# A transformer block's last batch: output tiles, the last pair's softmax sums, and the output gate, in another order

## The chip, the cores and the metric

The kernel runs on one core of one Trainium2 chip. The metric is the device time of one execution in microseconds (us), the median of several runs of the same program.

## What is computed

The reference is one block with adaptive layer norm, on an input of 8 batches, 1024 rows and 256 columns:

```python
h = _layernorm(x, axis=-1) * (1 + ca) + sa
x = x + ga * _L0_attn_ref(h, w_qkv, w_o)        # 16 heads of 64 columns
h = _layernorm(x, axis=-1) * (1 + cb) + sb
x = x + gb * _L0_ffn_ref(h, router_w, router_b, w1, b1, w2, b2)
```

`sa, ca, ga, sb, cb, gb` are six rows of 256 numbers for each batch. The attention is softmax(q k / 8) v for each head, then one product with `w_o`. The second part routes: a softmax over 8 experts for each of the 8192 rows, and each expert takes its 512 highest rows, applies two layers to them and adds the result, weighted by the score, to the output. So no expert can begin before every row of every batch has its score: the search for each expert's threshold needs all of them.

## The kernel before

**Attention.** A unit is one batch, one pair of heads and one half of 512 queries: 8 batches, 8 pairs, 2 halves, 128 units (`NSU`). Each has eight chunks of 128 keys. The work is written out by hand in steps `g`, four for a unit, in a loop (L732 on) that issues for each step: the subtraction of the row maxima (`subtract`, L425), the score products of a later unit (`scores_mm`, L360), exponentials (`exp_of`, L428) and value products (`values_mm`, L431) of a unit six steps back. Other work is put into these steps by `at(g, where, f, ...)` (L247), with places named load, m1, post, pool and m2, and is issued by `run` (L250). Each engine executes its instructions in the order issued; the SP queue too.

**Sums.** GpSimd adds up the eight exponential tiles of a unit (`add_up`, L449); `den_out` (L462) multiplies the sum by a matrix of ones (`den_mm`, L468: four 32-row products into one PSUM tile) and `den_store` (L478) copies it out and stores it to DRAM. When both halves of a pair are there, `den_load` (L492) reads the sums back as 128 rows, `den_inv` (L498) takes reciprocals and stores them, `den_spread` (L506) loads each as a broadcast over 64 partitions (`rb`), and `den_mul` (L514) multiplies the pair's transposed output `oT` by them, on GpSimd; on VectorE for the last pair of the last batch. `oT` goes to DRAM and comes back by tiles of 128 rows (`ot`), except for the last two pairs of the last batch (`at_hand`, L460), which stay in SBUF.

**Output of a batch, a tile of 128 rows at a time.** `out_proj` (L542): 16 products, over eight pairs, into one PSUM tile. `out_add` (L554): times the gate `ga` (L558, VectorE, `mods[b][:, 0]`), plus the residual (L559), store, statistics (L116, L117). `out_norm` (L563): 1/sqrt on GpSimd (`rstd_of`, L106, L108), scale (L571), times 1 + cb (L572) and plus sb (L573) on GpSimd. `out_turn` (L576): two tiles are transposed by products with the identity, in 64-column halves, and copied out (L590). `out_route` (L593): the logits of both tiles and their maximum. `out_exp` (L610), `out_score` (L618) and `out_store` (L628): the softmax over experts, a copy into `scores`, and a store of the row. For batches 0 to 6 these steps lie between the attention steps of the next batch.

**The last batch** has no attention to lie under, and is written out behind the loop (L771 to L823). For the last unit, `den_mm` isn't preceded by GpSimd's adding: four products for each chunk stand between the value products (L755 to L758). Behind the loop stand, in this order: the store, load, reciprocal and spread of the last pair's sums, the load of `mods` and of the residuals `xs` (L771 to L786); for each of eight tiles, the products of pairs 0 to 6 (L802 to L807); the product of the last pair's `oT` with the reciprocals (L808); for each tile, pair 7 (L809); and then one loop over the tiles, in which `out_add` of tile s, `out_norm` of tile s - 1 and the routing steps of earlier tiles follow each other:

```python
        for s in range(NT + 5):
            if s < NT:
                out_add(b, s, pos[s])
            if 1 <= s < NT + 1:
                out_norm(b, s - 1)
```

`last_load` (L641) loads `ot` for the last batch, six pairs of a tile at a time, at steps 515 and 516.

**Behind it**: the weights of four experts are loaded (`load_expert`), the scores are transposed (L889), and the threshold search runs 15 rounds on VectorE and TensorE (L899 to L924; L904 counts). Then the experts (L1083 to L1101).

Of the kernel before, what the change touches and what calls it, by code (L numbers as in the profile page):

```python
# [28 lines left out]
F32 = mybir.dt.float32  # L29
# [3 lines left out]
ALU = mybir.AluOpType  # L33
# [4 lines left out]
P = 128  # L38
# [4 lines left out]
def adaln_block(  # L43
# [15 lines left out]
    nc = tc.nc  # L59
# [418 lines left out]
    def den_store(u, pd):  # L478
        b, p, h = unit(u)
        den = small.tile([P, QH], F32, tag="den", name=f"den{u}", bufs=2)  # L480
        nc.scalar.copy(den, pd)
        if h == 0:
            den_d[b, p] = dram.tile([2, S], F32, name=f"den_d{b}_{p}")
        nc.sync.dma_start(
            den_d[b, p][:, h * QB : (h + 1) * QB].rearrange("j (i q) -> j i q", i=2),
            den[::32, :],
        )


    dens = {}  # L490
# [22 lines left out]

    def den_mul(b, p):  # L514
        oT = oTs.pop((b, p))
        if (b, p) == (B - 1, NP - 1):
            nc.vector.tensor_mul(oT, oT, dens.pop((b, p)))
        else:
            nc.gpsimd.tensor_tensor(oT, oT, dens.pop((b, p)), ALU.mult)  # L519
        if (b, p) in at_hand:  # L520
            at_hand[b, p] = oT
        else:
            nc.sync.dma_start(oT_d[b][p], oT)


    o_x, o_h, o_t = {}, {}, {}
# [49 lines left out]
    def out_turn(pool, b, t, tag="mm"):  # L576

        n = f"{b}_{t}"
        pt = pool.tile([P, 2, KC, P], F32, tag=tag, name=f"pth{n}")
        for i in range(2):  # L580
            h2 = o_h[b, t + i]
            for k in range(KC):
                for m in range(2):
                    c0 = k * P + m * N
                    nc.tensor.matmul(
                        pt[m * N : (m + 1) * N, i, k, :], h2[:, c0 : c0 + N], ident,
                        start=True, stop=True,
                    )
        h2T = small.tile([P, 2, KC, P], F32, tag="h2T", name=f"h2T{n}", bufs=1)
        nc.scalar.copy(h2T, pt)  # L590
        o_x[b, t] = h2T
# [44 lines left out]
    def gates(b):  # L636
        nc.sync.dma_start(
            rows_d[b * S : (b + 1) * S, ROW:], gb_d[b : b + 1, :].to_broadcast([S, D])
        )

    def last_load(t):  # L641
        b = B - 1
        o_t[b, t] = work.tile([P, NP - 2, P], F32, tag="p", name=f"ot{b}_{t}", bufs=PB)
        nc.sync.dma_start(
            o_t[b, t], oT_d[b][: NP - 2, :, t * P : (t + 1) * P].rearrange("n p s -> p n s")
        )
# [18 lines left out]
    for b in range(B):  # L665
        for p in range(NP):
            P0 = 8 * (b * NP + p)
            for i, g in enumerate((-7, -6, -5, -2)):
                if P0:
                    at(P0 + g, "m1", qk_task, b, p, i)  # L670
            if p % 2 == 0:
                for t, g in enumerate((-9, -3, -1, 5)):
                    if P0 or g > 0:
                        at(P0 + g, "m1", v_task, b, p // 2, t)
            if (b, p) == (B - 1, NP - 1):
                continue

            at(P0 + 17, "load", den_load, b, p)
            at(P0 + 18, "post", den_inv, b, p)
            at(P0 + 19, "load", den_spread, b, p)  # L680
            at(P0 + 20, "pool", den_mul, b, p)
        if b + 1 < B:
            if b + 2 < B:
                for t in range(NT // 2):
                    ln_task(b + 2, t, free_slot(64 * (b + 1) + 39 + 4 * t, True))
            for t in range(NT):
                g = free_slot(64 * (b + 1) + 19 + 4 * t, True)
                at(g - 2, "load", out_load, b, t)
                at(g, "m2", out_proj, ps_m, b, t)
                at(g + 1, "pool", out_norm, b, t)  # L690
                if t % 2:
                    g = free_slot(g + 2, True)
                    at(g, "m2", out_turn, ps_m, b, t - 1)
                    g = free_slot(g + 1)
                    at(g, "m2", out_route, ps_m, b, t - 1)
                    at(g + 1, "post", out_exp, b, t - 1)
                    at(g + 2, "post", out_score, b, t - 1)
                    at(g + 3, "pool", out_store, b, t - 1)
    for u in range(NSU):
        at(4 * u + 4, "m1", max_rows, u)  # L700
        if u < NSU - 1:
            at(4 * u + 12, "m2", den_out, u)
    for b in range(B):
        at(64 * b + 30, "load", gates, b)
    for i in range(2):
        at(2 + i, "m2", mod_rows, i)
    for t in range(NT):
        at(4 * NSU + (3 if t < NT // 2 else 4), "load", last_load, t)

    with tc.manual_schedule():  # L710
        first_loads()
# [20 lines left out]
        while g < 4 * NSU + LAG or steps:  # L732
            u, gm = divmod(g, 4)
            run(g, "load")
            if gm == 1 and 0 < u <= NSU:
                max_spread(u - 1)
            u1, gm1 = divmod(g - LAG + 1, 4)
            late = [(u1, 2 * gm1 + i) for i in range(2) if 0 <= u1 < NSU]

            for uc in late[: 1 if gm == 3 else 2]:  # L740
                subtract(*uc)
            if 0 <= u < NSU:
                for c in (2 * gm, 2 * gm + 1):
                    scores_out(u, c, scores_mm(u, c))
            if gm == 3 and late:
                subtract(*late[1])
            run(g, "m1")
            run(g, "post")
            for uc in late:
                exp_of(*uc)  # L750
            u1, gm1 = divmod(g - LAG, 4)
            if 0 <= u1 < NSU:
                for c in (2 * gm1, 2 * gm1 + 1):
                    values_mm(u1, c)
                    if u1 == NSU - 1:  # L755
                        if c == 0:
                            pd_last = ps_s.tile([P, QH], F32, tag="s", name="pd_last")
                        den_mm(pd_last, probs.pop((u1, c)), start=(c == 0), stop=(c == NT - 1))  # L758
                if gm1 == 3:
                    values_out(u1)  # L760
                if u1 < NSU - 1:
                    add_up(u1, gm1)
            if gm == 3 and 0 <= u < NSU:
                max_turn(u)
                split_max(u)
            run(g, "pool")
            run(g, "m2")
            g += 1


        b = B - 1  # L771
        den_store(NSU - 1, pd_last)
        den_load(b, NP - 1)
        den_inv(b, NP - 1)
        den_spread(b, NP - 1)
        mods[b] = work.tile([P, 3, D], F32, tag="mod", name=f"mod{b}", bufs=1)
        nc.sync.dma_start(
            mods[b].rearrange("p m d -> p (m d)"), mod_d[b : b + 1, :].to_broadcast([P, 3 * D])
        )
        for i in range(2):  # L780
            xs = work.tile([P, 4, D], F32, tag="p", name=f"xs{i}", bufs=PB)
            nc.sync.dma_start(
                xs, x[b, i * 4 * P : (i + 1) * 4 * P, :].rearrange("(t p) d -> p t d", p=P)
            )
            for t in range(4):
                o_x[b, 4 * i + t] = xs[:, t : t + 1, :]  # L786

        pos = []
        for pool, tag, n in (
            (ps_s, "s", 2), (ps_b, "less", 2), (ps_m, "mm", 1), (ps_av, "av", 1), (ps_s, "s", 2)  # L790
        ):
            po = pool.tile([P, n, 512], F32, tag=tag, name=f"po_last{len(pos)}")
            pos += [po[:, i, :D] for i in range(n)]

        def add_pair(t, p, src):
            for m in range(2):
                nc.tensor.matmul(
                    pos[t][m * N : (m + 1) * N, :], src[:, m * N : (m + 1) * N],
                    wo[:, p, :], start=(p == 0), stop=(p == NP - 1),
                )  # L800

        for t in range(NT):  # L802
            for p in range(NP - 1):
                if p < NP - 2:
                    add_pair(t, p, o_t[b, t][:, p, :])
                else:
                    add_pair(t, p, at_hand[b, p][:, t * P : (t + 1) * P])  # L807
        den_mul(b, NP - 1)  # L808
        for t in range(NT):  # L809
            add_pair(t, NP - 1, at_hand[b, NP - 1][:, t * P : (t + 1) * P])  # L810
        for s in range(NT + 5):
            if s < NT:
                out_add(b, s, pos[s])
            if 1 <= s < NT + 1:
                out_norm(b, s - 1)
            if s % 2 == 0 and 2 <= s < NT + 2:
                out_turn(*((ps_s, b, 0, "s") if s == 2 else (ps_m, b, s - 2)))
            if s % 2 and 3 <= s < NT + 3:
                out_route(ps_b, b, s - 3, tag="less")
                out_exp(b, s - 3)  # L820
            if s % 2 == 0 and 4 <= s < NT + 4:
                out_score(b, s - 4)
                out_store(b, s - 4)  # L823
    assert not steps, sorted(steps)
    attn.close()

# [306 lines left out]
```

## Time and profile before

| what | us |
|---|---|
| median of 3 runs | 3599.44 (3599.09 to 3600.59) |
| the profiled execution | 3597.83 |
| its span, first to last instruction | 3596.1 |
| TensorE busy in it | 3450.2 (96%) |
| VectorE, ScalarE, GpSimd busy | 2859.3, 2438.7, 2652.1 |
| last instruction of the attention loop's value products | 3212.6 |
| first count of the threshold search (L904) | 3272.6 |
| first product of the experts (L1049) | 3349.6 |

Times inside the execution are counted from the first instruction of the span. In the profile PE is TensorE's products, PEld its loading of weights, DVE VectorE, ACT ScalarE, POOL GpSimd, SP the queue that issues most transfers; "SPq" lines are its issues. An arrow names what was written and what was read, with buffer numbers left out. In the timeline a line gives start, duration, engine, line, operation, operands and count, and in brackets the idle time before it and what ended that. Instructions of the same kind that follow each other are merged into one line. A table by stretches gives for each one its length, then the busy time and number of instructions of each engine, the TensorE clock granted as a share of full speed, the busy share of the transfer engines and GB/s. The waits give who waited for whom, the total, how often, and the longest.

### The profile page before, as it was taken

To read this page: it belongs to the slowest core of one execution; us is meant where nothing else is said; L and a number is where in the kernel's file an instruction comes from. 1 tells how busy PE (TensorE), PEld (TensorE's weight loads), DVE (VectorE), ACT (ScalarE), POOL (GpSimd) and SP (SyncE) were. 2 spreads that over 40 slices of the span, in tenths; PEclk is the share of its full clock that TensorE was granted. 3 is DMA by queue.
4 is the path that set the end of the run, shared out by engine and by line. 5 is a ranking of instruction groups with operands and counts; after the bars stand their busy time and mean duration, and the time that the engine had idled before them with its cause. 6 is when DMAs were issued, how large, how long until landed. Compare 5 with 4: busy or idle time off the path is not lost. (4 is left out here: it accounts for less than half of the span.)

```text
span 3596.1 us, 54368 instructions
## 1 busy us (share of the span) xinstructions
PE 3450.2 (96%) x20718; PEld 1454.7 (40%) x20718; DVE 2859.3 (80%) x3618; ACT 2438.7 (68%) x2996; POOL 2652.1 (74%) x1537
## 2 busy tenths in 40 slices
PE   7999999999999999999999999999999999993898
PEld 3333333343433434334433343344433434442566
DVE  5888888888888888888888888988888888867432
ACT  4777777777777777777777777777777777750111
POOL 2778778888888887978788888887888788752233
PEclk9999999999999999999999999999999999995899
DMA  3020012011130112111211112111211112133342
GB/s 78 13 42 31 25 32 67 30 45 45 51 59 29 50 57 56 34 40 45 66 53 31 48 50 63 31 42 53 59 44 44 41 44 63 46 92 129 93 101 43
DMA packets 189653, 185.40 MB, mean 52 GB/s; under 512 B 48952, under 2 KB 167240, under 8 KB 189264
## 3 DMA queue, kind: packets, MB, share of 16 engines
q1 hardware_dynamic: 173616, 160.29, 16.3%
q0 software_dynamic: 7168, 12.72, 1.8%
q10 hardware_dynamic: 8608, 8.92, 0.8%
q8 instruction: 163, 2.67, 0.3%
q14 instruction: 98, 0.80, 0.1%
HBM read 127.06 MB, written 63.21 MB: 53 GB/s over the span
## 5 line engine op out<-in xcount | busy, mean ns | idle before, releaser
L457 POOL TENSOR_TENSOR acc<-acc,p 128x1024 f32<-128x1024 f32 x762 | 1805.3, 2369 | 362.4 <-ACT p L429 329.1
L376 ACT COPY p<-s 128x1024 f32<-128x1024 f32 x1024 | 995.8, 1018 | 419.1 <-PE s L367 412.1
L426 DVE TENSOR_TENSOR p<-p,less 128x1024 f32<-128x1024 f32 x1024 | 1206.7, 1210 | 32.6 <-PE less L423 30.1
L381 DVE TENSOR_TENSOR top<-top,s 128x1024 f32<-128x1024 f32 x768 | 936.8, 1220 | 276.3 <-ACT p L376 236.0
L429 ACT ACTIVATE p<-p 128x1024 f32<-128x1024 f32 x1024 | 1041.7, 1057 | 73.7 <-DVE p L426 73.3
L367 PE MATMUL s<-qk,qk 64*128 64x512 f32 x4096 | 1024.7, 612 | 34.0 <-DVE parts L404 31.0
L438 PE MATMUL av<-p,v 128*64 128x512 f32 x4096 | 967.2, 593 | 1.8 <-ACT oT L447 1.8
L367 PEld LDWEIGHTS s<-qk,qk 64*128 64x128 f32 x4096 | 358.8, 186 | 527.5 <-issue 240.9
L332 PE MATMUL pq<-hT,wq 128*64 128x512 f32 x2048 | 498.5, 608 | 2.7 <-ACT v L354 2.1
L438 PEld LDWEIGHTS av<-p,v 128*64 128x64 f32 x4096 | 280.6, 137 | 461.4 <-issue 366.2
L454 POOL TENSOR_TENSOR acc<-p,p 128x1024 f32<-128x1024 f32 x127 | 301.6, 2375 | 178.1 <-ACT p L429 178.1
L332 PEld LDWEIGHTS pq<-hT,wq 128*64 128x64 f32 x2048 | 124.8, 136 | 342.2 <-issue 210.8
L349 PE MATMUL pv<-wq,hT 128*64 128x256 f32 x2048 | 249.3, 386 | 0.7 <-ACT qk L337 0.7
L1053 ACT ACTIVATE h<-ph,b_sb 128x512 f32<-128x512 f32 (+1 forms) x72 | 46.0, 639 | 263.5 <-PE ph L1049 263.5
L396 DVE TENSOR_REDUCE tt<-tt 128x8 f32<-128x1024 f32 x128 | 157.4, 1230 | 69.9 <-PE tt L388 69.8
L548 PE MATMUL po<-wo,ot 128*64 128x256 f32 x1792 | 205.7, 382 | 0.0
L349 PEld LDWEIGHTS pv<-wq,hT 128*64 128x64 f32 x2048 | 135.7, 136 | 153.2 <-issue 65.9
L381 DVE TENSOR_TENSOR top<-p,s 128x1024 f32<-128x1024 f32 x128 | 155.8, 1217 | 14.0 <-ACT p L376 14.0
L388 PEld LDWEIGHTS tt<-ident,top 128*128 128x128 f32 x1024 | 109.6, 140 | 106.6 <-DVE top L381 105.8
L519 POOL TENSOR_TENSOR oT<-oT,rb 128x1024 f32<-128x1024 f32 x63 | 150.0, 2380 | 3.7 <-DMA rb<-rden_d 3.7
L548 PEld LDWEIGHTS po<-wo,ot 128*64 128x64 f32 x1792 | 123.5, 137 | 66.1 <-issue 9.4
L388 PE MATMUL tt<-ident,top 128*128 128x128 f32 x1024 | 139.9, 280 | 2.6 <-DVE top L381 2.6
(169 smaller groups left out, 2293.4 us busy)
## 6 DMA issues: line engine op xcount, KB each, us to landing
rb<-rden_d SPq DMA_DIRECT2D x128, 256.0 KB
oT_d<-oT SPq DMA_DIRECT2D x62, 512.0 KB
ot<-oT_d SPq DMA_DIRECT2D x56, 512.0 KB
rows_d<-row SPq DMA_DIRECT2D x64, 132.0 KB
rows_d<-gb_d SPq DMA_DIRECT2D x8, 1024.0 KB
w<-in_L_ffn_w_dram ACTq DMA_DIRECT2D x8, 1024.0 KB
w<-in_L_ffn_w_dram SPq DMA_DIRECT2D x8, 1024.0 KB
lnx<-in_L_attn_inputs_dram SPq DMA_DIRECT2D x28, 256.0 KB
```

The source lines that it names most:

```text
L332: nc.tensor.matmul(pq[m * N : (m + 1) * N, :], wq_of(k, a, 2 * p + m), hTs[b][:, k, sl], start=(k == 0), stop=(k == KC - 1),)
L349: nc.tensor.matmul(pv[m * N : (m + 1) * N, i, :], hTs[b][:, k, t0 : t0 + N], wq_of(k, 2, 4 * g, 4), start=(k == 0), stop=(k == KC - 1),)
L367: nc.tensor.matmul(ps[:, j, :], kt[r, c * P : (c + 1) * P], qt[r, h * QB : (h + 1) * QB], start=True, stop=True,)
L376: nc.scalar.copy(probs[u, c], ps)
L381: nc.vector.tensor_tensor(tops[u], probs[u, 0] if c == 1 else tops[u], ps, ALU.max)
L388: nc.tensor.transpose(turned[u][:, 4 * j + t, :], top[:, j, t * P : (t + 1) * P], ident)
L426: nc.vector.tensor_tensor(probs[u, c], probs[u, c], less[u], ALU.add)
L429: nc.scalar.activation(probs[u, c], probs[u, c], AF.Exp)
L438: nc.tensor.matmul(avs[u][j * N : (j + 1) * N, :], v[:, c, hh * N : (hh + 1) * N], pT[:, j, :], start=(c == 0), stop=(c == NT - 1),)
L454: nc.gpsimd.tensor_tensor(sums[u], pts[0], pts[1], ALU.add)
L457: nc.gpsimd.tensor_tensor(sums[u], sums[u], pt, ALU.add)
L548: nc.tensor.matmul(po[m * N : (m + 1) * N, :], ot[:, p, m * N : (m + 1) * N], wo[:, p, :], start=(p == 0), stop=(p == NP - 1),)
```

## The change

The loop of attention steps is the same up to step 508. In the last steps and behind the loop:

- The last unit's chunks 0 to 3 are added up by GpSimd like those of other units; the products with ones for chunks 4 to 7 and for that sum stand behind all value products, in another PSUM pool. The unit before gets its `den_out` one step earlier.
- The sums of the last pair are handled in halves of 512 queries: store, load, reciprocal, store, broadcast load and product for each half. Half 0 is issued on SP, half 1 on ScalarE's queue. Both products are VectorE's.
- `mods` of the last batch is loaded at step 510, and VectorE multiplies the output weights `wo` by the gate in two halves at step 516; the multiplication by the gate for each tile is gone.
- The scores of the tiles 6 and 7 of batch 6 are computed at step 516 instead of an earlier one (behind the last subtractions).
- Tiles 0 to 3 get pairs 0 to 6, then pair 7; each later tile gets its eight pairs in one piece, between the residuals, norms, turns, routes and softmaxes of earlier tiles, in an order written out as a list. Odd tiles' products with 1 + cb and sums with sb are VectorE's, even tiles' GpSimd's. The last batch's transposes are whole 128x128 ones.

```diff
+        if (b, p) == (B - 1, NP - 1):
+            dst = den_d[b, p, h] = dram.tile([2, QB], F32, name=f"den_d{b}_{p}_{h}")
...
+        eng = nc.scalar if u == NSU - 1 else nc.sync
+        eng.dma_start(dst.rearrange("j (i q) -> j i q", i=2), den[::32, :])
...
+    def last_load_den(h):
+        d = last_d[h] = small.tile([P, 2 * QB // P], F32, tag="dq", name=f"dq_last{h}", bufs=2)
+        (nc.scalar if h else nc.sync).dma_start(
+            d, den_d[B - 1, NP - 1, h].rearrange("j s -> (j s)").rearrange("(p c) -> p c", p=P)
+        )
+
+    def last_inv(h):
+        eng = nc.scalar if h else nc.sync
+        nc.vector.reciprocal(last_d[h], last_d[h])
+        rd = dram.tile([2, QB], F32, name=f"rden_last{h}")
+        eng.dma_start(
+            rd.rearrange("j s -> (j s)").rearrange("(p c) -> p c", p=P), last_d[h]
+        )
+        t = last_d[h] = work.tile([P, QB], F32, tag="p", name=f"rb_last{h}", bufs=PB)
+        for j in range(2):
+            eng.dma_start(
+                t[j * N : (j + 1) * N, :], rd[j : j + 1, :].to_broadcast([N, QB])
+            )
+
+    def last_mul(h):
+        half = oTs[B - 1, NP - 1][:, h * QB : (h + 1) * QB]
+        nc.vector.tensor_mul(half, half, last_d[h])
...
+                if b == B - 1:
+                    nc.tensor.transpose(pt[:, i, k, :], h2[:, k * P : (k + 1) * P], ident)
+                    continue
...
+    def last_gates():
+        n = NP // 2
+        for i in range(2):
+            w = wo[:, i * n : (i + 1) * n, :]
+            nc.vector.tensor_tensor(
+                w, w, mods[B - 1][:, 0, :].unsqueeze(1).to_broadcast([P, n, D]), ALU.mult
+            )
...
-            at(4 * u + 12, "m2", den_out, u)
+            at(4 * u + (12 if u < NSU - 2 else 11), "m2", den_out, u)
...
+    at(4 * NSU - 2, "load", last_mods)
...
+    at(4 * NSU + 4, "load", last_load_den, 0)
+    at(4 * NSU + 4, "pool", last_gates)
+    at(4 * NSU + 5, "post", last_inv, 0)
...
-                    if u1 == NSU - 1:
-                        if c == 0:
-                            pd_last = ps_s.tile([P, QH], F32, tag="s", name="pd_last")
-                        den_mm(pd_last, probs.pop((u1, c)), start=(c == 0), stop=(c == NT - 1))
...
-                if u1 < NSU - 1:
+                if u1 < NSU - 1 or gm1 < 2:
                     add_up(u1, gm1)
...
+        pd_last = ps_m.tile([P, QH], F32, tag="mm", name="pd_last")
+        for c in range(4, NT):
+            den_mm(pd_last, probs.pop((NSU - 1, c)), start=(c == 4), stop=False)
+        den_mm(pd_last, sums.pop(NSU - 1), start=False)
+        den_store(NSU - 1, pd_last)
+        last_load_den(1)
+        last_inv(1)
...
+        def add_x(t):
+            x1 = o_x[b, t]
+            nc.vector.tensor_add(x1[:, 0, :], x1[:, 0, :], pos[t])
+            nc.sync.dma_start(out[b, t * P : (t + 1) * P, :], x1[:, 0, :])
+            mv = stats_of(small, x1, 1, f"b{b}_{t}")
+            o_h[b, t] = mv, rstd_of(small, mv, 1, f"b{b}_{t}")
+
+        def norm(t):
...
+            eng = nc.vector if t % 2 else nc.gpsimd
+            eng.tensor_tensor(h2, h2, mods[b][:, 2, :], ALU.mult)
+            eng.tensor_tensor(h2, h2, mods[b][:, 1, :], ALU.add)
...
+        half = NT // 2
+        for t in range(half):
+            add_pairs(t, 0, NP - 1)
+        last_mul(0)
+        for t in range(half):
+            add_pairs(t, NP - 1, NP)
+        last_mul(1)
+        for f, *args in (
+            (add_x, 0), (add_x, 1), (norm, 0), (add_pairs, 4, 0, NP), (add_x, 2), (norm, 1),
+            (add_x, 3), (norm, 2), (add_pairs, 5, 0, NP), (turn, 0), (norm, 3), (add_x, 4),
+            (route, 0), (norm, 4), (add_pairs, 6, 0, NP), (turn, 2), (add_x, 5), (norm, 5),
+            (score, 0), (route, 2), (add_pairs, 7, 0, NP), (turn, 4), (add_x, 6), (norm, 6),
+            (score, 2), (add_x, 7), (route, 4), (norm, 7), (score, 4), (turn, 6), (route, 6),
+            (score, 6),
+        ):
+            f(*args)
```

`add_pairs(t, p0, p1)` issues the products of tile t for pairs p0 to p1 - 1 (the old `add_pair` in a loop over pairs); `turn` and `route` are `out_turn` and `out_route` in the pool of the score products; `score` is `out_exp`, `out_score` and `out_store` one behind the other.

## The prediction, made before the changed kernel ran

> **What bounds the kernel now.** I read the forty-slice view first: TensorE is full until slice 36, then 3, 8, 9, 8, so the change can only act in the tail of the attention part. Next the busy times by stretch:
>
> ```profile
> 3200.00:3213.00 13.00, 12.99 (x104) 3.10 (x104) 6.17 (x10) 7.20 (x10) 3.77 (x4) 1.00 0.78 195
> 3213.00:3237.00 24.00, 24.00 (x226) 16.00 (x224) 1.48 (x2) 0.57 (x2) 0.00 (x0) 1.00 0.55 143
> 3241.00:3247.00 6.00, 1.29 (x14) 1.01 (x16) 4.37 (x12) 0.00 (x0) 4.33 (x9) 0.74 0.19 63
> 3247.00:3254.00 7.00, 3.59 (x38) 2.53 (x34) 4.81 (x16) 1.08 (x3) 4.70 (x11) 0.50 0.18 59
> ```
>
> The columns are TensorE, weight loads, VectorE, ScalarE, GpSimd, then clock, DMA share, GB/s. From 3213 to 3237 TensorE alone works (the output products of eight tiles); from 3241 VectorE and GpSimd work and TensorE idles, half-clocked. Two phases stand one behind the other. The waits say what joins them:
>
> ```profile
> DVE at L558 <- PE po_last L797: 10.8, 1, 10.8
> PEld pth L585 <- POOL row L573: 14.0, 7, 2.9
> DVE oT L517 <- DMA rb<-rden_d: 6.1, 1, 6.1
> ```
>
> The first residual waits until every tile has pairs 0 to 6, though its operands are long there; then each transpose waits for GpSimd. The timeline gives the anchors:
>
> ```profile
> 3203.89 9.52 SPq L644 DMA_DIRECT2D ot<-oT_d  x8
> 3218.39 0.32 SPq L494 DMA_DIRECT2D dq<-den_d  x1
> 3226.34 1.23 DVE L517 TENSOR_TENSOR oT<-oT,rb 128x1024 f32<-128x1024 f32 x1 [6.13 <-DMA rb<-rden_d]
> 3238.37 0.42 DVE L558 TENSOR_TENSOR at<-po_last,mod 128x256 f32<-128x256 f32 x1 [10.81 <-PE po_last L797]
> 3242.04 0.72 DVE L559 TENSOR_TENSOR xs<-xs,at 128x256 f32<-128x256 f32 x1
> 3272.64 0.75 DVE L904 TENSOR_SCALAR_CACHE_REDUCE above<-sc,cand 128x512 f32<-128x512 f32 x1
> ```
>
> First residual at 3238.37, first count of the threshold search at 3272.64. Everything behind 3272.64 (323.5 us) is the same work before and after, so the question is where this anchor goes.
>
> **What the Trainium skill says.** "SBUF — State Buffer", section "Who interferes with whom": a VectorE instruction with two SBUF inputs and a GpSimd instruction that reads SBUF exclude each other for a whole instruction. The trace agrees: L559 takes 0.42 us alone and 0.72 across GpSimd's L572. "TensorE: Matmul & The Clock Gate", section "Part 1": an idle window of about 3.4 us halves the clock, a busy one restores it. The trace agrees: 1.00 falls to 0.50 at about 3244, 3 us after the dense products, and returns at 3353.1, 3.5 us after the experts' products begin at 3349.6. "DMA: Bandwidth & Descriptors", section "Issuing engines are not separate DMA queues": transfers of two queues run on the same 16 engines; a second queue saves issue time only. No row here shows it for the last pair.
>
> **The change part by part.**
>
> *Sums behind the values.* Eight groups of den_mm stood between the values at about 0.57 us each (start to start in the timeline, 3201.01 to 3201.58); now five groups of 0.5 (p4 to p7, and the GpSimd sum of p0 to p3) stand behind them. The values then wait for the exponentials instead: VectorE's last subtraction ends near 3205.6 (the score instructions, 0.76, moved behind it; before 3206.24), the last exponential near 3206.9, the last value product near 3207.9, the sums near 3210.4. GpSimd takes on three adds of 2.38 us, 3201.1 to 3208.4, before its oT product (then to 3210.8, before 3210.3). So the output products start near 3210.5 instead of 3213.06.
>
> *Gates in the output weights.* Two VectorE products of 128x1024, 1.23 us each by L517's row, before the first output product; they remove eight 0.42 us multiplications (L558) and turn L559's two-SBUF-input add into one that reads PSUM. Nobody waits if they end by 3210.5: uncontended 3208.9. With the lock against GpSimd's adds and oT product each may wait up to one 2.37 us instruction: up to 3213. I take 3211; a late start is covered, because TensorE waits at pair 7 anyway (next step). Without that cover it costs up to 2.5 us. The `mod` load moved to group 510 is one 0.57 us issue on SP, which was idle until 3196.
>
> *Halves on two queues.* SP's order is now: four ot loads, den store of half 0, four ot loads, dq load, reciprocal's store, rb, row stores, xs. The ot loads fill SP and the engines (DMA share about 1.2 from 3207 to 3217; the packets end near 3218.3), so the dq load of half 0, issued near 3214, lands behind them, near 3218.6. From here the trace of before has the whole chain: dq issue 3218.39, landed 3219.96, rb issue 3221.68, product 3226.34. So: reciprocal 3218.9, rb issue 3220.6. Both rb halves (ScalarE's queue carries the other, and its reciprocal stands behind half 0's on VectorE) together are the bytes of the old rb: 2.9 us of packets, 3221.9 to 3224.4 for half 0. The added waits: on SP, half 0's reciprocal store also waits for the landing of half 1's den store (they share a completion counter in the built program; ScalarE issues that near 3211, landed near 3213: no wait, but rb, rows and xs stand behind it); on ScalarE, four waits for transfers up to 3221.8, with nothing behind them before the first copy of a transpose near 3233; on VectorE, half 1's reciprocal stands ahead of product 0, its load issued near 3213 and landed near 3215. Product 0 is 0.62 us (half of L517): ends 3225.2. TensorE has done four tiles of pairs 0 to 6 (3.02 us each in the timeline, 12.1 together) by 3222.6 to 3224, waits 1 to 3 us, and starts pair 7 at 3225.3. Two tiles of it (0.86) and the 0.4 us that L558 saw behind its last product: 3226.6. xs must be there as well: SP issues it after rb and two row stores, near 3222.6; its packets follow those of rb and rows: first half landed near 3227.3. First residual **3227.3** instead of 3238.37: 11.1 us gained. Bounds: 3225.2 if dq isn't last behind the slowest engine and xs overlaps; 3230 if xs needs the 8.1 us from the first rb packet that it took before.
>
> *Tile by tile.* TensorE's remaining work is in VectorE's shadow: tiles 4 and 5 (3.45 each) end 7.4 us behind tile 3's pair 7; turn (0.55 now, whole transposes), copy (0.6), route (0.6) fit between. VectorE, with the timeline's pitches: add, statistics, aggregate 1.03 a tile; scale 0.3; an odd tile's two products 0.92, up to 1.5 against GpSimd's pair (0.75 each); logits 0.4 and scores 0.85 a pair; mean to rstd and back 1.05 (3246.28 to 3247.30). Laid out in the order of the built program from residual 0: tiles 0 to 3 normalised at 9.25 (two lock waits), residuals 4 and 5 from 9.25 and 11.6 (1.4 us of waits for rstd), tile 5 done 15.45, scores 0 at 16.25, residual 6 at 16.65, residual 7 at 20.15, tile 7 scaled at 22.25 and done 23.55. Then the serial end: before it took 8.4 us from the last scale (3264.24) to the count; minus 0.7 (two VectorE products for two GpSimd ones) and 0.3 (two transposes for four), 7.4. Sum **29.7 us**, before 34.3: 4.6 gained. Floor: without VectorE's waits 26; ceiling: before's pace, 34.
>
> *Clock.* The clock still falls before the last turn, as it did; I count the last turn at half speed. The experts' products begin at another place in the 3.4 us window, so the half-clocked stretch of 3.5 us may be up to 3.4 longer: 0 to 1.7 us lost, 0.6 at most gained; I take 0.5 lost.
>
> **Sum.** New anchor 3227.3 + 29.7 = 3257.0, 15.6 earlier; 0.5 back; 15.1 gained. The profiled execution took 3597.83 (span 3596.1 and 1.7 around it): 3582.7. The median of the runs, 3599.44, lies 1.6 higher: **3584**.
>
> **Rivals.**
> - *Loads set the start.* xs lands at 3230 as its old pace says, and lock waits take 2 us of the chain's gain: 8.4 + 2.6 = 11 gained, less clock: 3589. For it: VectorE waited 13.7 us for dq and 6.1 for rb, all behind ot. Against it: `mod`, the slowest of the old packets, is out of this stretch.
> - *Both waits short.* Start 3225.2, VectorE near its floor: 13.2 + 8 gained: 3579. Against it: GpSimd and VectorE need each other's results every tile.
> - *The lock eats it.* Odd tiles' eight products and eight score scalings each blocked by a whole GpSimd instruction (0.72): 11.5 back, 3595, no measurable change. Against it: GpSimd is free during half of them.
> - *Slower: the clock stays down.* If TensorE's wait at pair 7 fills a 3.4 us window and the stop-and-go of turn, copy, route never fills a busy one, its 20 us of remaining products take 40, with 2 us of copies: residual 7 then follows some 37 us behind pair 7's start, and the anchor 9.6 behind that: 3225.3 + 46.6 = 3272, all gain gone; each us of that wait comes on top, with up to 1.7 in the experts. It decides from a wait over 3.4 us; with 7 more (3232) the kernel ends near 3607. Against it: my wait is under 3, tiles 4 and 5 are 6.9 us without a stop.
>
> That the change doesn't do what it says is excluded: in the built order residual 0 waits only for tiles 0 and 1.
>
> **Chances.** Forecast 3584 (3580 to 3588): 0.60. Loads 3589 (to 3592): 0.18. Both short 3579: 0.13. Lock 3595: 0.05. Clock 3607: 0.04. The range 3578 to 3591 leaves out lock, clock and the ends of two cases, under 0.2. About 0.2% (7 us) is what measurement tells from no change: faster 0.90 (the first three, less a little of the loads' upper end), within 0.06, slower 0.04.
>
> **What would show it.** Right: first residual near 3227, an rb wait before a short product near 3224.6, L904's first count near 3257, TensorE dense to about 3243 with VectorE busy beside it, the experts unchanged in length but for the clock. Wrong: dq or xs landing past 3230; two-input products of VectorE at 0.7 and more throughout; a clock of 0.5 before 3243; output products starting after 3213.

## The result, and the profile after

| | before | after |
|---|---|---|
| median of 6 runs each, us | 3599.09 | 3585.86 (3584.34 to 3587.42) |
| ratio, 95% interval | | 0.9963 (0.9952 to 0.9975) |
| profiled execution, us (span) | 3597.83 (3596.1) | 3586.92 (3585.2) |
| copy of the last pair's first half of values, L447 | 3199.39 | 3202.08 |
| first residual of the last batch, L558 / L855 | 3238.37 | 3232.30 |
| first count of the search, L904 / L979 | 3272.64 | 3261.88 |
| first count to the end of the span | 323.46 | 323.32 |

The kernel became 0.37% faster, 13.2 us; the forecast, 3584, is missed by 1.9 us and the range, 3578 to 3591, holds. The profiled execution gained less, 10.9 us, and the table says why. Nothing that the copy of L447 waits for was changed, yet that copy falls 2.69 us later after than before. The difference arises in the first 40 us: here are the busy times from 28 to 35 us of before,

```profile
28.00:35.00 7.00, 6.95 (x24) 2.06 (x24) 1.21 (x1) 2.51 (x4) 0.00 (x0) 0.76 0.65 4
```

and of after, the same stretch.

```profile
28.00:35.00 7.00, 5.78 (x14) 1.90 (x16) 0.00 (x0) 1.66 (x3) 0.00 (x0) 0.51 0.68 4
```

The sixth figure behind the length is TensorE's clock, 1.00 at full speed: nearly all of these seven us are half-clocked here, about half of them in before's execution. It isn't the change that does this. Of the 14 profiles in this study, seven have a mean clock of 0.76 in this stretch, and the copy then falls at 3199.1 to 3199.8; the other seven have 0.51 to 0.63, and the copy falls at 3200.8 to 3202.1. The changed kernel, profiled twice, gave one of each. So I measure from the copy on. From the copy to the first count, "the stretch" below, before takes 73.25 us and after **59.80**: 13.45 gained, and 0.14 behind it. Times below are also given as distances from the copy.

The busy times by stretch of after answer those of before (columns as there):

```profile
3212.70:3226.00 13.30, 12.44 (x116) 7.86 (x112) 3.16 (x3) 0.37 (x1) 2.96 (x3) 1.00 0.72 172
3226.00:3228.70 2.70, 0.12 (x2) 0.00 (x0) 0.69 (x1) 0.00 (x0) 0.00 (x0) 1.00 0.99 277
3228.70:3233.10 4.40, 4.35 (x26) 2.61 (x28) 1.45 (x3) 0.00 (x0) 0.00 (x0) 0.62 0.65 201
3233.10:3240.00 6.90, 6.78 (x62) 4.28 (x58) 5.88 (x17) 0.09 (x1) 5.15 (x11) 1.00 0.24 79
3240.00:3252.00 12.00, 9.99 (x120) 6.74 (x120) 7.99 (x26) 2.45 (x7) 5.46 (x13) 1.00 0.17 56
```

The two phases now overlap: from 3233 to 3252 TensorE, VectorE and GpSimd work side by side at full clock. A hole has opened ahead of that, 3226.0 to 3228.7: apart from one VectorE instruction at its end almost nothing computes, the DMA engines are full, and behind it TensorE runs half-clocked (0.62 in the mean). Two of the waits inside the chain:

```profile
DVE row L864 <- POOL rs_b L108: 4.6, 5, 1.5
...
PEld pth L610 <- POOL row L869: 1.2, 1, 1.2
```

The 10.8 us wait for pairs 0 to 6 is gone, and of the 14.0 us of transposes waiting for GpSimd 1.2 are left (2.5 more are a wait for VectorE). In their place stand three loads one behind the other: dq (the sums), the spread, and xs. The timeline shows them, with VectorE's wait for each in brackets (the wait of L549 carries the name of a row store that landed last; the operand that it needs is rb_last, the spread):

```profile
3206.52 3.85 SPq L689 DMA_DIRECT2D ot<-oT_d  x4
...
3211.29 4.51 SPq L689 DMA_DIRECT2D ot<-oT_d  x4
3215.89 1.17 SPq L530 DMA_DIRECT2D dq_last<-den_d  x1
...
3223.78 1.11 SPq L543 DMA_DIRECT2D rb_last<-rden_last  x2
...
3226.09 1.12 SPq L820 DMA_DIRECT2D xs<-in_L_attn_inputs_dram  x2
...
3222.06 0.38 DVE L536 RECIPROCAL dq_last<-dq_last 128x8 f32<-128x8 f32 x2 [6.58 <-DMA dq_last<-den_d]
3228.00 0.69 DVE L549 TENSOR_TENSOR oT<-oT,rb_last 128x512 f32<-128x512 f32 x1 [5.56 <-DMA rows_d<-row]
...
3232.30 0.42 DVE L855 TENSOR_TENSOR xs<-xs,po_last 128x256 f32<-128x256 f32 x1 [2.66 <-DMA xs<-in_L_attn_inputs_dram]
...
3228.75 2.77 PE L847 MATMUL po_last<-wo,oT 128*64 128x256 f32 x16 [2.64 <-DVE oT L549]
...
3250.08 0.66 PE L610 MATMUL pth<-ident,row 128*128 128x128 f32 x4
```

First residual at 30.22 us behind the copy (before 38.98): 8.76 gained. From there to the first count 29.58 us, "the chain" (before 34.27): 4.69 gained. The last line is the third of the four turns, at 48.00 behind the copy; it matters below.

### The profile page after: what moved, and what is told of

The parts are those of the page before. It is cut to its first block, busy times and chain, and to the rows that moved or that the text cites. A ratio compares the mean times of both kernels' runs of the same rounds, so it can differ in the third digit from the quotient of the medians.

```text
span 3585.2 us, 54232 instructions
## 1 busy us (share of the span) xinstructions
PE 3445.0 (96%) x20646; PEld 1450.6 (40%) x20646; DVE 2866.0 (80%) x3622; ACT 2439.5 (68%) x2996; POOL 2655.4 (74%) x1532
## 5 line engine op out<-in xcount | busy, mean ns | idle before, releaser
L339 ACT COPY qk<-pq 128x512 f32<-128x512 f32 x128 | 75.0, 586 | 99.6 <-PE pq L332 99.6
```

## The experiments

My theory: the overlap moved the residuals forward; what now sets their start is the loads, xs last; TensorE's wait at pair 7 and its clock lie beside the path. Rivals: TensorE and the clock set the start; one part of the change alone gained the chain's 4.7 us; sums, halves and queues do nothing. All runs, from one profile each (stretch, first residual and third turn from the copy on) and the timed executions:

| run | first residual | chain | stretch | third turn | TensorE's wait at pair 7 | median, us |
|---|---|---|---|---|---|---|
| after | 30.22 | 29.58 | 59.80 | 48.00 | 2.64 | 3585.86 |
| after again | 29.84 | 30.29 | 60.13 | 48.11 | 2.73 | 3584.88 |
| xs early | 30.49 | 32.30 | 62.79 | 50.99 | 4.37 | 3587.50 |
| gates back | 27.55 (product with the gate) | 34.21 | 61.76 | 47.76 | 3.32 | 3587.66 |
| GpSimd for all tiles | 30.06 | 30.91 | 60.97 | 48.39 | 3.01 | 3586.69 |
| whole pair | 30.47 | 32.18 | 62.65 | 50.85 | 4.35 | 3589.08 |
| sums back | 30.36 | 29.75 | 60.11 | 46.45 | 0.71 | 3584.66 |
| xs early, warm | 29.03 | 30.36 | 59.39 | 47.49 | filled | 3584.47 |
| old order | 37.09 | 25.95 | 63.04 | other order | none | 3588.03 |
| ot late | 30.83 | 30.27 | 61.10 | 48.86 | none | 3586.81 |
| loads reordered | 25.37 | 30.02 | 55.39 | 43.47 | none | 3580.68 |
| reordered, sums back | 27.30 | 30.96 | 58.26 | 45.85 | 0.22 | 3584.34 |
| quartered turns | 30.17 | 31.37 | 61.54 | 49.00 | 3.27 | 3586.47 |

Against before, the ratios of the two ends are 0.9950 (0.9936 to 0.9963, loads reordered) and 0.9972 (0.9962 to 0.9981, whole pair). The intervals of neighbours overlap, so the verdicts rest on the stretches; two profiles of the same kernel differ by 0.33 us there.

**xs early.** Does xs set the start?

```diff
     at(4 * NSU + 4, "load", last_load_den, 0)
+    for i in range(2):
+        at(4 * NSU + 4, "load", last_x, i)
```

(last_x holds the xs load that stood behind the loop.)

> The two xs loads are issued on SP directly behind half 0's dq load, ahead of its wait for the reciprocal; all else as in the changed kernel. Measured from the copy of the last pair's first half of values (L447) to the search's first count, 59.80 us in the changed kernel. Theory (the loads set the start, xs last): VectorE's first residual no longer waits 2.66 us for xs; it waits for TensorE's pair 7 of tiles 0 and 1, which began at 3228.75 and reads at half clock, so the residual moves 1.9 to 2.3 us earlier and the stretch is 57.5 to 58. Rival (start set by TensorE and the clock, xs just a companion): stretch 59.8 +-0.4. Rival 2 (bytes only trade places: xs ahead pushes dq or rb back by its own 2.5 us): 60 or more.

The first residual came 0.27 us later, not 1.9 earlier: the bytes traded places. xs stood ahead of the reciprocal's store and the spread, and product 0 began 27.66 us behind the copy instead of 25.92. This is the second rival, with a surprise: the stretch grew by 3.0 us although the residual hardly moved. TensorE's line and the busy times of this run show why:

```profile
3229.82 3.68 PE L851 MATMUL po_last<-wo,oT 128*64 128x256 f32 x16 [4.37 <-DVE oT L549]
...
3252.40 0.66 PE L610 MATMUL pth<-ident,row 128*128 128x128 f32 x4
```

```profile
3229.00:3232.00 3.00, 2.18 (x10) 1.24 (x12) 1.40 (x3) 0.00 (x0) 0.00 (x0) 0.50 0.02 6
3232.00:3235.00 3.00, 3.00 (x17) 1.66 (x15) 2.83 (x9) 0.00 (x0) 1.58 (x4) 0.50 0.26 87
3235.00:3238.00 3.00, 3.00 (x28) 1.89 (x26) 2.86 (x7) 0.00 (x0) 2.45 (x5) 0.87 0.13 44
```

A wait of 4.37 us halved the clock from 3229.0 to 3235.8 (0.87 over three us is 0.8 us at half), twice as long as in after (the half-clocked stretches at pair 7 in these profiles last 3.4 or 6.8 us, one or two "windows"). Tiles 0 to 3's pair 7 took 3.68 us instead of 2.77, everything behind it on TensorE was late, and the third turn moved by 2.99 us, exactly as far as the stretch. Of that, 1.74 us is pair 7's later start (28.41 us behind the copy instead of 26.67) and 1.25 the longer time at half clock. So TensorE is not beside the path in the chain; that part of my theory fell here.

**Gates back.** Which part shortened the chain?

```diff
-    at(4 * NSU + 4, "pool", last_gates)
...
-            nc.vector.tensor_add(x1[:, 0, :], x1[:, 0, :], pos[t])
+            tmp = small.tile([P, D], F32, tag="at", name=f"at{b}_{t}", bufs=2)
+            nc.vector.tensor_mul(tmp, pos[t], mods[b][:, 0, :])
+            nc.vector.tensor_add(x1[:, 0, :], x1[:, 0, :], tmp)
```

> Undoes the gates in the output weights alone: no product of the weights with the gate; each of the eight tiles again multiplies by the gate from PSUM (0.42 us) and adds the residual with two SBUF operands (0.42 to 0.72). Theory (the gates are what shortened the chain from residual 0 to first count): chain 29.6 becomes 33.3 to 35, so the stretch from the copy L447 to the first count is 63.5 to 65 instead of 59.80; the first residual itself stays within 0.5 us. Rival (the chain is shorter through the odd/even split and whole transposes; TensorE's tiles and the rstd waits cover VectorE): chain at most 31, stretch at most 61.2.

The stretch grew by 1.96 us: more than the rival allowed and well under the 3.7 to 5.2 of the theory. The timeline shows one of the eight products hidden under the wait for xs:

```profile
3228.84 0.42 DVE L855 TENSOR_TENSOR at<-po_last,mod 128x256 f32<-128x256 f32 x1 [0.58 <-PE po_last L846]
3230.95 0.42 DVE L856 TENSOR_TENSOR xs<-xs,at 128x256 f32<-128x256 f32 x1 [1.68 <-DMA xs<-in_L_attn_inputs_dram]
```

The other seven are 3.2 us of VectorE at a pitch of 0.45, the adds with two SBUF operands 0.5 us more (0.479 us in the mean against 0.411; the lock was cheap here). Against that, VectorE's waits for rstd, logits and exponentials fell from 6.8 to 5.8 us, and the first add came 0.56 us earlier: 3.7 − 1.6 is the 2.0 measured, nearly.

**GpSimd for all tiles.**

```diff
-            eng = nc.vector if t % 2 else nc.gpsimd
+            eng = nc.gpsimd
```

> Undoes the split alone: GpSimd does the two norm products of all eight tiles, as before, VectorE none. Theory: VectorE loses 4 x 0.92 us of work but the odd tiles wait for GpSimd behind the even ones; every VectorE row with two SBUF inputs still meets the lock. GpSimd has 16 x 0.73 us, 11.7 us, under the 20 us between first and last scaling, so it isn't the bound on average; the last tile's two products stand 0.6 us longer in the serial end. Chain 29.6 becomes 29 to 31. Rival (the split is what gained the 4.7 us): chain 32 to 34, stretch from the copy L447 to the first count 62.2 to 64 instead of 59.80.

Chain 30.91, stretch 1.17 longer (0.84 against after's second profile): the theory. The split is worth about one us; it didn't gain the 4.7.

**Whole pair.**

```diff
-        last_load_den(1)
-        last_inv(1)
+        den_load(b, NP - 1)
+        den_inv(b, NP - 1)
+        den_spread(b, NP - 1)
...
-        last_mul(0)
+        oT = oTs[b, NP - 1]
+        nc.vector.tensor_mul(oT, oT, dens.pop((b, NP - 1)))
...
-        last_mul(1)
...
```

(half 0's own load and reciprocal go, and the xs loads stand behind the spread, as they did.)

> Undoes the halves and the second queue alone: one dq load, one reciprocal, one store, one spread and one product of 128x1024 for the last pair, all on SP (ScalarE issues only the den store of half 1, as in the changed kernel). Theory (the loads share the engines and both halves landed together, so halves and the second queue gain only the product's 0.6 us, which hides behind xs): first residual within 0.7 us of the changed kernel, stretch from the copy L447 to the first count 59.5 to 60.8. Rival (halves on two queues are what made the start early): dq waits for half 1's den store on SP's side and the spread takes twice as long to issue: stretch 62 or more.

The first residual stayed within 0.25 us, as the theory said, but the stretch grew by 2.85, in the rival's range by another way. The product began 1.2 us later behind the copy and took 1.23 us instead of 0.69; so TensorE waited 4.35 us, took the same 3.68 us for pair 7, and its third turn moved by 2.85 us. Halves and the second queue together are therefore worth something: not for the residual, but because they keep TensorE's wait short. (In this run two row stores also stand ahead of the sums' load on SP, so a part of the 1.2 us may be theirs.)

**Xs early, warm.** Is it the clock? Eighteen products whose results are overwritten fill the wait.

```diff
             add_pairs(t, 0, NP - 1)
+        for i in range(9):
+            for m in range(2):
+                nc.tensor.matmul(
+                    pos[7][m * N : (m + 1) * N, :], at_hand[b, NP - 2][:, m * N : (m + 1) * N],
+                    wo[:, i % NP, :], start=True, stop=True,
+                )
         last_mul(0)
```

> The kernel with early xs loads and, ahead of pair 7, eighteen products that write a PSUM tile which tile 7's first product overwrites: they fill 3.9 of the 4.37 us that TensorE waited there. Theory (that wait was over one clock window, which cost two windows, 6.8 us, at half clock and so made TensorE the bound of the chain): the clock stays at 1.00 to about 3253, pair 7 of four tiles takes 1.75 instead of 3.68 us, the chain from residual 0 to first count falls from 32.3 to 29.0 to 30.2, and the stretch from the copy L447 from 62.79 to 58.5 to 60.5. Rival (the chain was longer for another reason, such as VectorE's waits for ScalarE): chain within 0.7 us of 32.3.

```profile
3229.00:3232.00 3.00, 3.00 (x32) 1.99 (x30) 2.82 (x9) 0.00 (x0) 1.75 (x5) 1.00 0.29 93
```

The clock stayed at 1.00 here and until 3251, the stretch fell from 62.79 to 59.39, chain 30.36 (0.16 above the expected range). The spread was also 0.56 us faster in this run (product 0 at 27.10 behind the copy); that leaves 2.8 us for the clock.

**Sums back.**

```diff
                     values_mm(u1, c)
+                    if u1 == NSU - 1:
+                        if c == 0:
+                            pd_last = ps_s.tile([P, QH], F32, tag="s", name="pd_last")
+                        den_mm(pd_last, probs.pop((u1, c)), start=(c == 0), stop=(c == NT - 1))
...
-                if u1 < NSU - 1 or gm1 < 2:
+                if u1 < NSU - 1:
...
```

(the sums behind the loop go.)

> Undoes the sums behind the values alone: the eight groups of den_mm for the last unit stand between its value products again, and GpSimd makes no partial sum of it. Stretch from the copy L447 of the last pair's first half to the first count: 59.80 us in the changed kernel. Theory (TensorE waits 2.6 us at pair 7 anyway, so output products that start 2.5 us later cost nothing, and a shorter wait can spare one half-clocked window): 58.5 to 60.3. Rival (moving the sums gained the 2.5 us by which the output products start earlier): 61.8 to 62.8.

Stretch 60.11: nothing lost, though the output products start 3.0 us later (13.68 behind the copy instead of 10.65). TensorE's wait at pair 7 took the delay up:

```profile
PE po_last L847 <- DVE oT L549: 0.7, 1, 0.7
```

This run says something else too. The clock stayed full and the third turn came 1.55 us earlier than in after, yet the chain is 29.75. So VectorE's own order, with its waits for GpSimd, needs these 29.7 us, as the prediction had laid it out; in after TensorE merely arrives about level with it.

**Old order.**

```diff
-        half = NT // 2
-        for t in range(half):
+        for t in range(NT):
             add_pairs(t, 0, NP - 1)
...
+        for s in range(NT + 5):
+            if s < NT:
+                add_x(s)
+            if 1 <= s < NT + 1:
+                norm(s - 1)
...
```

> Undoes the order alone: pairs 0 to 6 of all eight tiles, then pair 7 of all, then residuals, scalings, turns, routes and scores in the order of before; gates in the weights, the split and the halves stay. Theory (the overlap of the output products with VectorE's tail gained some 6 to 9 us): first residual 36.5 to 37.5 us behind the copy L447 instead of 30.2, chain 27 to 30, stretch to the first count 64 to 67 instead of 59.80. Rival (VectorE's chain alone sets it and merely starts later but runs faster without TensorE's tiles in the way): stretch 60 to 62.

The first residual went to 37.09, as expected, on this wait:

```profile
DVE xs L855 <- PE po_last L847: 9.8, 1, 9.8
```

But the chain took only 25.95 us, less than expected and the floor that the prediction gave for VectorE without waits, and the stretch grew by 3.2 us alone, between both expectations. Before's chain in the same order took 34.27: gates, split and whole turns together are worth 8.3 us when nothing else is in the way, and the overlap gives 3.6 of that back: in after VectorE waits 4.6 us for mean and rstd, a wait that this run doesn't have, and TensorE's tiles stand between its turns. Against before this run gained 10.2 us from the copy on. So most of the change's 13.4 us needs no new order of the tiles; the order adds 3.2.

**Ot late.**

```diff
-    for t in range(NT):
-        at(4 * NSU + (3 if t < NT // 2 else 4), "load", last_load, t)
+    for t in range(NT // 2):
+        at(4 * NSU + 3, "load", last_load, t)
...
+        for t in range(NT // 2, NT):
+            last_load(t)
```

> Moves the ot loads of tiles 4 to 7 on SP behind the spread of half 0 and behind xs; nothing else. Theory (the start is set by what the sums' small loads queue behind): dq lands 4 us earlier or more, the spread near 3220, TensorE doesn't wait at pair 7 (under 0.5 us) and its clock stays at 1.00; first residual 25.3 us behind the copy L447 instead of 30.2, chain 29 to 30, stretch to the first count 54 to 56. Rival (latency of each hop, not the queue ahead of it, sets dq and rb): first residual moves by under 1.5 us, stretch over 58. Rival 2 (the tiles' loads then come late for TensorE): a wait of TensorE for ot of tile 4.

```profile
3220.80 0.69 DVE L549 TENSOR_TENSOR oT<-oT,rb_last 128x512 f32<-128x512 f32 x1 [6.46 <-DMA rb_last<-rden_last]
3229.59 0.69 DVE L549 TENSOR_TENSOR oT<-oT,rb_last 128x512 f32<-128x512 f32 x1 [8.09 <-DMA rb_last<-rden_last]
3230.20 0.41 DVE L857 TENSOR_TENSOR xs<-xs,po_last 128x256 f32<-128x256 f32 x1
...
3228.62 4.11 PE L849 MATMUL po_last<-wo,ot 128*64 128x256 f32 x24 [3.45 <-DMA ot<-oT_d]
```

The first half of the theory holds: product 0 at 21.43 behind the copy instead of 25.92, 4.5 us earlier, and no wait at pair 7. The gain was lost twice. Half 1's spread, on ScalarE's queue, was issued only at 3221.04, behind the completion of a row store of SP (both name the same semaphore in the trace), and its packets then ran among those of ot; product 1 stands ahead of the residuals on VectorE and held them to 3230.20. And TensorE waited 3.45 us for tile 4 (the second rival).

**Loads reordered.** The version that these runs point to: first xs half into the gap while SP waits for the reciprocal's store, ot of tiles 4 to 7 behind the spread, product 1 behind residual 1.

```diff
         )
+        if h == 0:
+            last_x(0)
         t = last_d[h] = work.tile([P, QB], F32, tag="p", name=f"rb_last{h}", bufs=PB)
...
+        if h == 0:
+            for i in range(NT // 2, NT):
+                last_load(i)
+            last_x(1)
...
-        last_mul(1)
         for f, *args in (
-            (add_x, 0), (add_x, 1), (norm, 0), (add_pairs, 4, 0, NP), (add_x, 2), (norm, 1),
+            (add_x, 0), (add_x, 1), (last_mul, 1), (norm, 0), (add_pairs, 4, 0, NP), (add_x, 2), (norm, 1),
...
```

(the loads of ot for tiles 4 to 7 at step 516 and of xs behind the loop go.)

> SP's order for the last batch becomes: ot of tiles 0 to 3, den store, dq and reciprocal's store of half 0, first xs half, spread of half 0, ot of tiles 4 to 7, second xs half; and product 1 stands on VectorE behind residuals 0 and 1 instead of ahead of them. Theory (small loads behind big ones set the start, and a wait at pair 7 also cost clock): no wait of TensorE over 0.5 us at pair 7 or for ot, clock 1.00 until the dense products end; first residual 24.5 to 25.5 us behind the copy L447 (30.2 in the changed kernel), chain to the first count 29 to 30.5, stretch 54 to 56; median some 4 to 5 us under the changed kernel's of the same chip. Rival (the first xs half gets in the way of the spread by its own 2.9 us): TensorE waits 1 to 3 us at pair 7 and the stretch is 57 to 60.

```profile
3214.60 0.38 SPq L703 DMA_DIRECT2D xs<-in_L_attn_inputs_dram  x1
3217.22 1.11 SPq L545 DMA_DIRECT2D rb_last<-rden_last  x2
3218.42 2.96 SPq L695 DMA_DIRECT2D ot<-oT_d  x4
...
3222.89 2.33 PE L855 MATMUL po_last<-wo,oT 128*64 128x256 f32 x20
3225.05 2.76 PE L855 MATMUL po_last<-wo,ot 128*64 128x256 f32 x24
```

TensorE doesn't stop from the second tile to the sixth, the first residual falls at 25.37, the stretch is 55.39. Median 3580.68, 4.2 us under the changed kernel's on the same chip and 0.5% under before. This is the theory of the loads in full: it takes the order of three kinds of load, and product 1 behind residual 1, to bring 4.4 to 4.7 us of the stretch (against after's two profiles).

**Reordered, sums back.** The edit of "sums back" on top.

> The reordered loads as in the run before, with the last unit's eight sums between its value products again and no GpSimd partial sum. Theory (the sums behind the values cost nothing to undo in the changed kernel only because TensorE waited at pair 7; without that wait TensorE's dense run carries the end): stretch from the copy L447 to the first count 2.0 to 2.7 us longer than in the run before. Rival (sums in between are hidden in any case, or GpSimd's three adds cost as much as they save): within 0.7 us of it.

2.87 us longer, 3.7 in the median: slightly more than expected. Without the wait at pair 7 nothing covers TensorE's later start (3.03 us).

**Quartered turns.**

```diff
-                if b == B - 1:
-                    nc.tensor.transpose(pt[:, i, k, :], h2[:, k * P : (k + 1) * P], ident)
-                    continue
```

> Undoes the whole transposes alone: each tile of the last batch is turned by four products of 64 columns again instead of two of 128. Theory (TensorE has slack between turns in the changed kernel, so only the last turn, at half clock, counts): chain 29.6 becomes 29.8 to 30.5, stretch 59.8 becomes 60.0 to 60.9. Rival (turns and the ScalarE copy behind them pace the chain): stretch 61.5 or more.

Stretch 61.54, 1.4 to 1.7 us longer, just in the rival's range, though 0.3 to 0.4 of that is a longer wait at pair 7. A turn took 1.04 us instead of 0.66: the two ahead of the third put it off by 0.6 us, and the end behind it grew by 0.5 to 0.7. I had given TensorE slack between the turns; it has none.

**After again.** The changed kernel unedited.

> The changed kernel itself once more, on the chip of the reordered one. Theory: stretch from the copy L447 to the first count 59.3 to 60.5 wherever the copy itself falls, so differences of one to three us in the time come from before that copy or behind the first count. Rival (the wait at pair 7 sometimes takes two clock windows instead of one): stretch 61.5 to 62.8 in this run.

60.13, with the copy at 3199.76 this time, near before's 3199.39: the theory. It ran 2.04 us faster than the first profiled execution, as the copy says.

**What paces the chain.** VectorE shows where TensorE comes in: at the sums over the exponentials of tiles 2 and 3. In after and, below it, in xs early:

```profile
3251.84 0.17 DVE L651 TENSOR_REDUCE rd<-ex 128x2 f32<-128x16 f32 x1 [0.36 <-ACT ex L644]
...
3254.15 0.17 DVE L651 TENSOR_REDUCE rd<-ex 128x2 f32<-128x16 f32 x1 [2.04 <-ACT ex L644]
```

ScalarE's timeline of after shows what those exponentials stand behind:

```profile
3250.83 0.59 ACT L619 COPY h2T<-pth 128x512 f32<-128x512 f32 x1 [4.48 <-PE pth L610]
3251.31 0.49 ACT L644 ACTIVATE ex<-lg,rnm 128x8 f32<-128x8 f32 x2
```

The exponentials of tiles 2 and 3 (their logits were ready at 3249.1) stand on ScalarE behind the copy of the third turn, which stands on TensorE behind tile 7's products; on VectorE the scores of tiles 2 and 3 stand ahead of residual 7. So residual 7 waits for TensorE by way of an unrelated exponential. VectorE's wait there is 0.36 us in after, 0.84 in its second profile, 2.04 in both xs early and whole pair, and 1.78 with quartered turns; in every run that has it the first count follows the third turn by 11.8 to 12.6 us, wherever that turn falls. Sums back and gates back don't have it (13.66 and 14.00 us from the third turn to the count): where TensorE comes early or VectorE has more to do, VectorE's own order sets the end. Loads reordered and its variant (11.92 and 12.41) list no such wait either, but there the exponentials ended within 0.2 us of VectorE's coming. This is read from the traces; no run moved that exponential, so what moving it would gain is not shown.

## Why the prediction was right, step by step

Times in before's frame (after's, less 2.69).

- *Sums behind the values*: output products at 3210.04, predicted 3210.5. Worth nothing in this kernel (sums back, 0.0 to 0.3 us), as the step said with its cover, and 2.9 once that cover is gone.
- *Gates*: the second product ended at 3212.8 instead of 3211, at the upper bound: it took 3.38 us, across GpSimd's product of oT. TensorE waited 0.86 us; covered. On the stretch they bring 2.0 (gates back).
- *Halves on two queues*: every hop a little late: reciprocal 3219.4 (3218.9), spread issued 3221.1 (3220.6), product 0 ended 3226.0 (3225.2), pair 7 started 3226.1 (3225.3). TensorE's wait 2.64, inside the 1 to 3.
- *First residual*: 3229.6 instead of **3227.3**, 8.8 gained instead of 11.1. This is the mis-sized term. I let xs follow the spread with the pace of its bytes, 4.7 us from issue to landing; it was issued at 3223.4 instead of 3222.6, with the packets of both spreads and of the row stores ahead of it, and the residual that waits for it began 6.2 us later, near the upper bound of 3230. The rival "Loads set the start" had the better size for this term; its other half, a lock that takes 2 us of the chain, did not come.
- *Chain*: 29.58 and 30.29, predicted 29.7. The size is right, and so is VectorE's layout: behind the first residual, residuals 4, 5, 6 and 7 follow at 9.53, 11.90, 16.74 and 20.22 us (predicted 9.25, 11.6, 16.65 and 20.15), and sums back, where TensorE is early, gives the same chain. The reason "TensorE's remaining work is in VectorE's shadow" is only just true: TensorE ends about level, and where it came later the stretch grew as much as or more than its third turn moved (xs early, whole pair, quartered turns). That the half-clocked window, which the prediction didn't have, stayed within this margin was luck.
- *Clock*: the experts lost about nothing (dense products half-clocked for 3.7 us, before 3.5), predicted 0.5. What I priced at nothing was the wait at pair 7: at 2.64 us, short of the 3.4 from which I thought that it decides, the clock fell all the same for one window, and "TensorE dense" was so only at a mean clock of 0.62 over 4.4 us. (The lines of before were also read loosely here: the clock fell 3.6 us behind the last dense product, not 3.) The slower rival had the mechanism, not the size: waits of 4.35 and 4.37 us brought a second window, the stretch grew by 2.85 and 2.99 us with 1.7 us of later start in it, and the clock then returned.

The sum, 15.1, became 8.8 + 4.7 + 0.1 = 13.6 from the copy on: the start's 2.3 too little, the experts' 0.5 and 0.2 of small terms too much. The second profile gives 9.1 + 4.0. The median fell by 13.2. The prediction added the earlier start and the shorter chain as two gains; old order shows that the overlap trades one for the other: without it the start comes 6.9 us later and the chain is 3.6 us shorter.

## What to carry to other kernels

A phase that was overlapped gains less than its length: undoing the order alone cost 3.2 us of the 13.4, since engines that overlap wait for each other. Where small loads in a chain of hops meet large ones, look at the order of issue before adding a queue (here reordering brought 4.4 to 4.7 us, halves and a second queue together 2.5 to 2.9), and follow each moved load to its own reader: ot late won 4.5 us for product 0 and lost them at two other readers. Look for instructions of another tile that stand between a producer and its reader on an in-order engine (here an exponential behind a copy behind a turn): through them an engine with apparent slack sets the end.

## What the runs showed of the hardware

An idle time of 2.64 us was enough for one half-clocked window of TensorE, though TensorE was busy for 0.98 of the 3.41 us ahead of the fall; the Trainium skill, "TensorE: Matmul & The Clock Gate", section "Part 1", asks for an idle window of about 3.4 us. Here the measurement decides: with 0.71 us (sums back) the clock stayed at 1.00, waits of 2.64 to 3.45 us brought one half-clocked window, 4.35 and 4.37 brought two. Where the half-clocked window began also differed: in quartered turns 0.3 us ahead of the wait's end, in ot late 1.4 us behind it. What share of a window must be idle stays open.

Small instructions of VectorE can wait long for GpSimd: two scalings of eight elements a partition took 2.48 us beside a GpSimd add of 128x1024 and ended with it, at 3211.0; with GpSimd idle the same two took 0.36 us.

```profile
3208.57 2.48 DVE L655 TENSOR_SCALAR row<-ex,rd 128x8 f32<-128x8 f32 x2
...
3248.47 0.36 DVE L655 TENSOR_SCALAR row<-ex,rd 128x8 f32<-128x8 f32 x2
```
